# Last attention layer of a four-layer network: the decay table's first step on VectorE, its bias and causal mask on GpSimd, and another order of calls per step

## Chip, cores and metric

The kernel runs on one core of a Trainium2 chip, in one launch. The metric is the device time in microseconds (us) of that launch. Everything is float32. The engines are TensorE (PE in the profile; its weight loads are PEld), VectorE (DVE), ScalarE (ACT), GpSimd (POOL) and the queue SP, which issues DMAs.

## What is computed

Four layers, each a normalisation, an attention, a feed-forward part and a gated sum, over 8 sequences of 512 tokens with 128 channels. The change lies in the attention of the last layer, which the kernel computes for 16 heads of 64 complex channels. Cut to what matters (`B_`=8, `N_`=512, `H_`=16, `DH_`=64):

```python
ang = t[:, None, None] * om[None]
phase = jax.lax.complex(jnp.cos(ang), jnp.sin(ang))
qr = q * phase[None]
kr = k * phase[None]
dt = jnp.abs(t[:, None] - t[None, :])
E = jnp.exp(jnp.clip(-mu[:, None, None] * dt[None], MIN_EXP, 0.0))      # MIN_EXP = -30
s = jnp.einsum('bihd,bjhd->bhij', qr, jnp.conj(kr)).real
V = (sigma_sq / (2.0 * mu))[:, None, None] * (1.0 - E * E) + (eta_sq + gamma_sq)[:, None, None]
maha = jnp.maximum(qn[..., None] + (E * E)[None] * kn[:, :, None, :] - 2.0 * E[None] * s, 0.0) / V[None]
coef = (-0.5 * tau * (nu + DH_))[None, :, None, None]
logits = coef * jnp.log1p(maha / nu[None, :, None, None]) - 0.5 * DH_ * jnp.log(V)[None]
logits = jnp.where(causal[None, None], logits, -jnp.inf)
A = jax.nn.softmax(logits, axis=-1)
out = jnp.einsum('bhij,bjhd->bihd', A.astype(v.dtype), v)
y = jnp.concatenate([out.real.reshape(B_, N_, DKt), out.imag.reshape(B_, N_, DKt)], axis=-1)
return y @ Wo
```

E and V depend on the head and on the distance of two tokens alone, not on the sequence.

## The kernel before

`l3_attention` holds one 512 x 512 causal score matrix as four row tiles of 128 rows with 128, 256, 384 and 512 columns, packed side by side: 1280 columns on 128 partitions. `off` gives the place of each row tile and `w` its width, so the square that the diagonal crosses is the last 128 columns of each row tile. Everything per score is an instruction of 1280 columns, or four instructions, one for each row tile, in the order 3, 2, 0, 1.

**Tables.** For each head, `class Tables` makes three tiles of 128 x 1280, two buffers each. `decay` writes E = max(nmu * dt, -30) on GpSimd, `exp` takes its exponential on ScalarE; `squares` (G = E * E), `variance` and `variance_nu` (V) are GpSimd's; `log` takes ln G on ScalarE; `bias` is one VectorE instruction, G = G * g_v + later, where `later` is a tile made once, 0 where the key is not later than the query and -1e30 elsewhere. So G carries the bias and the causal mask into the logits. A new `Tables` also issues the DMAs of the head's two weights and of its cosines and sines. The first head's tables are made at once, beside the layer norm in front of the attention; those of heads 1 to 15 by the entries "T..." of the step.

**Pairs.** The 128 pieces of work (16 heads x 8 sequences) are taken two sequences at a time: 64 objects of `class Pair`, x = 0 or 1 being the sequence. In the order of the data:
- `project` (PE, keys then queries), `rotate` (DVE: r2 = sin * psum, DMA of r2 to rs with the partition halves exchanged, r = cos * psum), `turned` (GpSimd: r = r + rs), `squares` (ACT), `key_norms`, `query_norms` (PE), `key_lengths` (ACT), `query_lengths` (DVE), `key_terms` (GpSimd: ek = E * kn, four instructions).
- `scores` (PE), `halved` (DVE: sc = -2 sc + ek), `scaled` (DVE: sc = sc * E), `distances` (DVE, four instructions, y = max(sc + qn, V)), `log` (ACT, both x at once), `logits` (DVE, both x: y = coef * y + G, 2560 columns, two inputs in SBUF).
- `maxima i` (DVE, row tile i of both x), `exps x i` (ACT), `inverse` (DVE), `values` (PE, the value and output weights already multiplied) and `keep_values` (ACT), `turn` (PE transposes) and `keep` (ACT), `weigh` (PE, 10 products, 20 passes), `normalise` (ACT), `add` (GpSimd, into the sum over heads). `finish` turns the sum back for the last head.

**Order.** `STEP` is a list of 72 calls. Step t runs it once: "1 scores 0" calls `scores(0)` of pair t+1, "-1 keep 0 2" calls `keep(0, 2)` of pair t-1, and "T2 variance" runs in every fourth step, where t % 4 is 2, for the next head. `in_order` fixes each engine's instructions to that order; the engines wait for each other by semaphores. So one call's place in the list sets only what it stands behind on its own engine, and the DMAs of `rotate` and of a new `Tables` keep their order on SP.

**Buffers that matter.** PSUM: one tile for scores (`s`), one for projections (`kq`), one for weighted sums (`o`), two (`j`) shared in turn by norms, transposes and values. SBUF: one r2, one rs, one sq; two of r, ek, kn, y, o, u and at.

Below, "step" is one run of the list, (n, x) in brackets is pair t+n and sequence x.

Of the kernel before, what the change touches and what calls it, by code (L numbers as in the profile page):

```python
# [9 lines left out]
F32 = mybir.dt.float32  # L10
I32 = mybir.dt.int32
AF = mybir.ActivationFunctionType
ALU = mybir.AluOpType
# [3 lines left out]
P = 128  # L17
# [6 lines left out]
NEG = -1.0e30  # L24
# [1284 lines left out]
def l3_attention(net, x, xn, s_out):  # L1309
    nc, tc = net.nc, net.tc  # L1310
    H, DH = 16, 64
    NQ = S // P
    PK = P * NQ * (NQ + 1) // 2


    w = [P * (i + 1) for i in range(NQ)]
    off = [896, 1024, 512, 0]
    banks = [(0, 512, (3,)), (512, 512, (2, 0)), (1024, 256, (1,))]
    with ExitStack() as st:
        p1 = st.enter_context(tc.tile_pool(name="a3_1", bufs=1))  # L1320
# [4 lines left out]
        sp, nmu, v_e2, v_0, coef, k_0, q_0, g_v = net.prep.scalars  # L1325
# [2 lines left out]
        wvo = p1.tile([P, H, P], F32, tag="wvo", name="wvo")  # L1328

        dt = p1.tile([P, PK], F32, tag="dt", name="dt")  # L1330
        later = p1.tile([P, PK], F32, tag="later", name="later")
        nc.gpsimd.memset(later, 0.0)
        with tc.tile_pool(name="a3_d", bufs=1) as pd:
            di = pd.tile([P, PK], I32, tag="di", name="di")
            for i in range(NQ):
                cols = slice(off[i], off[i] + w[i])
                nc.gpsimd.iota(di[:, cols], pattern=[[-1, w[i]]], base=P * i, channel_multiplier=1)
                nc.gpsimd.affine_select(
                    out=later[:, cols], in_=later[:, cols], compare_op=ALU.is_ge, fill=NEG,
                    base=P * i, pattern=[[-1, w[i]]], channel_multiplier=1,  # L1340
                )
            nc.vector.tensor_copy(dt, di)
        nc.vector.scalar_tensor_tensor(dt, dt, -1.0, dt, ALU.mult, ALU.max)

# [3 lines left out]
        pe, dve, act, pool = (  # L1348
            net.in_order(e) for e in (nc.tensor, nc.vector, nc.scalar, nc.gpsimd)
        )  # L1350
# [8 lines left out]
        class Tables:  # L1359


            def __init__(self, h):
                self.h, self.hs = h, slice(h, h + 1)
                for nm in "qk":
# [14 lines left out]
                nc.sync.dma_start(self.sn[96:128, :], sin)  # L1379
                self.E, self.V, self.G = (  # L1380
                    pw.tile([P, PK], F32, tag=nm, name=nm) for nm in "EVG"
                )

            def decay(self):
                pool.tensor_scalar(self.E, dt, nmu[:, self.hs], -30.0, ALU.mult, ALU.max)

            def exp(self):
                table_set("exp_and_others")
# [2 lines left out]
            def squares(self):  # L1391
                pool.tensor_tensor(self.G, self.E, self.E, ALU.mult)

            def variance(self):
                G = self.G
                pool.tensor_scalar(G, G, v_e2[:, self.hs], v_0[:, self.hs], ALU.mult, ALU.add)

            def variance_nu(self):
                G = self.G
                pool.tensor_scalar(self.V, G, nu[:, self.hs], 1.0, ALU.mult, ALU.mult)  # L1400

# [2 lines left out]
                act.activation(self.G, self.G, AF.Ln)  # L1404

            def bias(self):
                G = self.G
                dve.scalar_tensor_tensor(G, G, g_v[:, self.hs], later, ALU.mult, ALU.add)

        tables = {}  # L1410
        T = tables[0] = Tables(0)
# [2 lines left out]
        with tc.tile_pool(name="a3_v", bufs=2, space=PSUM) as p_v, tc.tile_pool(  # L1414
            name="a3_vw", bufs=2
# [24 lines left out]
        class Pair:  # L1440
# [185 lines left out]


        STEP = (
            "0 scores 1", "-1 exps 0 3", "1 key_lengths 0", "-1 exps 0 0", "-1 turn 0 2",
            "T1 decay", "0 halved 1", "-1 keep 0 2", "1 key_terms 0", "1 query_norms 0",  # L1630
            "-1 turn 0 0", "-1 exps 1 0", "-2 normalise 1", "1 query_lengths 0", "1 project 1 0",
            "1 turned 0", "0 scaled 1", "-1 exps 1 1", "-1 turn 0 1", "0 distances 1",
            "-1 keep 0 0", "1 project 1 1", "-2 add 0", "-1 keep 0 1", "1 rotate 1", "-1 weigh 0",
            "-1 inverse", "-1 turn 1 2", "0 log", "-1 turn 1 1", "0 logits", "T3 log",
            "1 scores 0", "T3 bias", "0 maxima 2", "-1 keep 1 2", "1 squares 1", "-1 keep 1 1",
            "0 values 0", "1 turned 1", "1 key_norms 1", "-1 normalise 0", "2 project 0 0",
            "0 keep_values 0", "1 halved 0", "1 key_lengths 1", "1 query_norms 1", "0 maxima 1",
            "-1 turn 1 0", "1 query_lengths 1", "T2 variance", "2 project 0 1", "0 exps 0 1",
            "0 values 1", "1 key_terms 1", "-1 keep 1 0", "T2 variance_nu", "-2 add 1", "T1 exp",
            "-1 weigh 1", "1 scaled 0", "2 squares 0", "0 maxima 3", "0 exps 1 2", "T1 squares",  # L1640
            "0 exps 1 3", "1 distances 0", "2 rotate 0", "2 key_norms 0", "0 keep_values 1",
            "0 exps 0 2", "0 maxima 0",
        )
        for t in range(-2, N + 3):
            if t + 2 < N:
# [391 lines left out]
def network(tc, ins, out):  # L2037
    with ExitStack() as ctx:
        net = Net(ctx, tc, ins)
        xp = ctx.enter_context(tc.tile_pool(name="acts", bufs=1))  # L2040
        x = xp.tile([P, NT], F32, tag="x", name="x")
        for t in range(NTB):
            tc.nc.sync.dma_start(x[:, ts(t, TB)], ins["x"][:, ts(t, TB)])
        xn = xp.tile([P, NT], F32, tag="xn", name="xn")
        s = xp.tile([P, NT], F32, tag="s", name="s")
        prep = net.prep = Prepared(net, ctx)
        with tc.tile_pool(name="prep_0", bufs=1) as p0:
            net.layer_norm(x, xn)
            l0_attention(net, xn, s)
            prep.l0_decode(p0)  # L2050
            l0_ffn(net, x, xn, s)
        net.layer_norm(x, xn)
        l1_layer(net, x, xn, s)
        net.layer_norm(x, xn)
        with tc.tile_pool(name="prep_t", bufs=1) as pt:
            prep.l2_weights(pt)
            l2_attention(net, xn, s)
            prep.angles(pt)
            prep.l3_scalars()
            l2_ffn(net, x, xn, s)  # L2060
            prep.sines()
        l3_attention(net, x, xn, s)
        l3_ffn(net, x, xn, s, out)
# [76 lines left out]
```

## Time and profile before

| what | us |
|---|---|
| runs of the kernel | 2869.78, 2870.13, 2882.57; median 2870.13 |
| the profiled execution's own time | 2865.32 |
| its span in the trace | 2863.6 |
| attention of the last layer, steady part (first to last `logits`) | 1361.3 to 2683.1 |
| from the last `logits` to the first work after the attention | 2683.1 to 2713.6 |

The span is what the trace covers; 1.7 us of the execution lie around it. In the trace all the calls of `STEP` carry line 82, that of the helper `in_order`, so that instructions are told apart by their tiles: `y<-y,coef,G` is `logits`, `G<-G,g_v,later` is `bias`, `E<-dt,nmu` is `decay`, `s<-s,o` is `add` (the sum over heads lies in s), `r<-r,rs` is `turned`, `ek<-E,kn` is `key_terms`. A row of a timeline reads: start, duration, engine, line, operation, output<-inputs, number of instructions, and in square brackets how long the engine was idle before it and what ended that. Successive VectorE instructions overlap by about 0.09 us, so durations add up to slightly more than the time they take.

### The profile page before, as it was taken

How to read it: one execution, taken by the hardware profiler on the slowest of the kernel's cores; microseconds unless marked ns; L12 is line 12 of the kernel's file. 1: busy time of each engine (PE TensorE's matmuls, PEld its weight loads, DVE VectorE, ACT ScalarE, POOL GpSimd, SP SyncE). 2: the span in 40 equal slices, each digit the busy share in tenths (PEclk: the TensorE clock that was granted, in tenths of full speed). 3: DMA queues.
4: the chain of work that ended last, by engine and by line, in shares of the span. 5: the costliest groups of instructions: out<-in, count | busy, mean ns of one | idle time of the engine just before them, and what ended most of it. 6: DMA issues, size and time to landing. Idle time of an engine off the chain costs nothing. (4 is left out here: it accounts for less than half of the span.)

```text
span 2863.6 us, 48763 instructions
## 1 busy us (share of the span) xinstructions
PE 2575.9 (90%) x18636; PEld 1801.4 (63%) x18636; DVE 2195.4 (77%) x2907; ACT 1835.7 (64%) x3587; POOL 1556.8 (54%) x1262
## 2 busy tenths in 40 slices
PE   7999898688778889977999999999999999999887
PEld 5666666455335555535677777677777777777674
DVE  4777454566663666664999999999999999999565
ACT  2666342245331455452899888898888889888734
POOL 2444221532342333335677877877877787777323
PEclk7999797899898899877999999999999999999989
DMA  1000002112100000003222222222222222222000
GB/s 48 2 2 2 1 1 89 30 51 46 32 28 17 2 2 2 2 23 92 62 61 57 49 62 61 61 61 57 54 57 61 62 56 66 55 52 52 25 1 30
DMA packets 56310, 112.73 MB, mean 39 GB/s; under 512 B 10768, under 2 KB 28752, under 8 KB 55440
## 3 DMA queue, kind: packets, MB, share of 16 engines
q1 hardware_dynamic: 51584, 99.40, 13.2%
q0 software_dynamic: 4352, 8.92, 1.3%
q8 instruction: 148, 2.42, 0.4%
q10 hardware_dynamic: 144, 1.31, 0.1%
q14 instruction: 82, 0.67, 0.1%
HBM read 30.43 MB, written 12.06 MB: 15 GB/s over the span
## 5 line engine op out<-in xcount | busy, mean ns | idle before, releaser
L82 POOL TENSOR_TENSOR ek<-E,kn 128x512 f32<-128x512 f32 (+3 forms) x512 | 427.1, 867 | 63.2 <-ACT kn L82 62.1
L82 POOL TENSOR_TENSOR r<-r,rs 128x1024 f32<-128x1024 f32 x128 | 317.9, 2484 | 252.9 <-DMA rs<-r 213.1
L82 POOL TENSOR_TENSOR e<-e,mx 128x1024 f32<-128x1024 f32 x112 | 212.6, 1898 | 333.8 <-DVE mx L82 195.5
L82 ACT ACTIVATE y<-y,mx 128x256 f32<-128x256 f32 (+3 forms) x512 | 287.2, 562 | 101.2 <-DVE mx L82 101.1
L82 PE MATMUL sc<-r 128*128 128x512 f32 (+3 forms) x1024 | 307.9, 444 | 24.6 <-POOL r L82 18.8
L82 PEld LDWEIGHTS ps_av<-u,at 128*128 128x128 f32 x2560 | 302.3, 193 | 41.2 <-ACT at L82 31.3
L82 PE MATMUL ps_av<-u,at 128*128 128x128 f32 x2560 | 315.1, 279 | 6.5 <-ACT at L82 6.5
L82 PEld LDWEIGHTS sc<-r 128*128 128x128 f32 x1024 | 166.4, 192 | 176.5 <-issue 71.7
L82 DVE SCALAR_TENSOR_TENSOR y<-sc,qn,V 128x512 f32<-128x512 f32 (+3 forms) x512 | 246.0, 543 | 2.3
L82 ACT ACT_TABLE_LOAD x167 | 214.3, 1283 | 4.1 <-PE pa L82 1.2
L82 DVE TENSOR_REDUCE mx<-y 128x2 f32<-128x768 f32 (+3 forms) x256 | 207.7, 812 | 1.7
L82 DVE SCALAR_TENSOR_TENSOR sc<-sc,ek 128x1280 f32<-128x1280 f32 x128 | 191.3, 1495 | 12.5 <-PE sc L82 6.2
L82 PE MATMUL tp<-ident,y 128*128 128x128 f32 x1280 | 198.5, 278 | 1.2 <-ACT y L82 0.8
L82 DVE SCALAR_TENSOR_TENSOR y<-y,coef,G 128x2560 f32<-128x2560 f32 x64 | 195.7, 3058 | 4.6 <-ACT y L82 2.3
L82 ACT COPY at<-tp 128x512 f32<-128x512 f32 (+1 forms) x384 | 188.2, 512 | 7.8 <-PE tp L82 7.7
L82 DVE TENSOR_TENSOR sc<-sc,E 128x1280 f32<-128x1280 f32 x128 | 191.1, 1493 | 0.0
L82 PEld LDWEIGHTS tp<-ident,y 128*128 128x128 f32 x1280 | 154.3, 146 | 41.4 <-issue 18.3
L82 POOL TENSOR_TENSOR s<-s,o 128x512 f32<-128x512 f32 x120 | 162.6, 1356 | 31.1 <-ACT o L82 31.1
L82 PEld LDWEIGHTS ps_u<-wvo,xn 128*128 128x128 f32 x1024 | 128.3, 191 | 69.2 <-DVE qn L82 55.2
L82 DVE TENSOR_TENSOR r<-sn,ps_kq 128x1024 f32<-128x1024 f32 x128 | 154.9, 1210 | 7.6 <-ACT sq L82 4.1
L82 ACT ACTIVATE y<-y 128x2560 f32<-128x2560 f32 x64 | 149.7, 2339 | 15.6 <-DVE y L82 8.1
L82 PE MATMUL tp<-ident,e 128*128 128x128 f32 x896 | 135.0, 294 | 23.6 <-ACT rt L82 14.4
(396 smaller groups left out, 5779.4 us busy)
## 6 DMA issues: line engine op xcount, KB each, us to landing
rs<-r SPq DMA_DIRECT2D x256, 256.0 KB
yrows<-yy SPq DMA_DIRECT2D x36, 128.0 KB
ct<-trig SPq DMA_DIRECT2D x16, 256.0 KB
m_w<-m_w SPq DMA_DIRECT2D x1, 2560.0 KB
x<-x SPq DMA_DIRECT2D x8, 256.0 KB
xrows<-row SPq DMA_DIRECT2D x8, 256.0 KB
sn<-trig SPq DMA_DIRECT2D x32, 64.0 KB
sn<-trig SPq DMA_DIRECT2D x16, 128.0 KB
```

Source lines behind the costliest of these rows:

```text
L82: ins = op(*args, **kwargs)
```

## The change

`decay` goes from GpSimd to VectorE, with the same operands. `bias` goes from one VectorE instruction to five on GpSimd: a product with g_v over all 1280 columns, then on the last 128 columns of each row tile an affine select, which keeps a score where row >= column and writes -1e30 elsewhere. `later`, its memset and its four selects go. `STEP` has the same 72 calls with the table calls at other steps ("T0 decay", "T0 exp" where it was T1) and another order; it starts at another point of the cycle.

```diff
-        later = p1.tile([P, PK], F32, tag="later", name="later")
-        nc.gpsimd.memset(later, 0.0)
         with tc.tile_pool(name="a3_d", bufs=1) as pd:
             di = pd.tile([P, PK], I32, tag="di", name="di")
             for i in range(NQ):
                 cols = slice(off[i], off[i] + w[i])
                 nc.gpsimd.iota(di[:, cols], pattern=[[-1, w[i]]], base=P * i, channel_multiplier=1)
-                nc.gpsimd.affine_select(
-                    out=later[:, cols], in_=later[:, cols], compare_op=ALU.is_ge, fill=NEG,
-                    base=P * i, pattern=[[-1, w[i]]], channel_multiplier=1,
-                )
...
             def decay(self):
-                pool.tensor_scalar(self.E, dt, nmu[:, self.hs], -30.0, ALU.mult, ALU.max)
+                dve.tensor_scalar(self.E, dt, nmu[:, self.hs], -30.0, ALU.mult, ALU.max)
...
             def bias(self):
+
                 G = self.G
-                dve.scalar_tensor_tensor(G, G, g_v[:, self.hs], later, ALU.mult, ALU.add)
+                pool.tensor_scalar(G, G, g_v[:, self.hs], 1.0, ALU.mult, ALU.mult)
+                for i in range(NQ):
+                    last = G[:, off[i] + P * i : off[i] + P * i + P]
+                    pool.affine_select(
+                        out=last, in_=last, compare_op=ALU.is_ge, fill=NEG,
+                        base=0, pattern=[[-1, P]], channel_multiplier=1,
+                    )
...
         STEP = (
+            "1 project 0 1", "0 key_terms 1", "-1 maxima 3", "-2 weigh 1", "-1 values 1",
+            "-1 exps 0 1", "1 squares 0", "-1 exps 1 1", "-1 exps 1 2", "1 key_norms 0",
+            "-1 keep_values 1", "-1 exps 0 3", "0 distances 0", "0 scores 1", "-1 exps 1 3",
+            "-1 turn 0 2", "1 key_lengths 0", "-1 exps 0 2", "-1 keep 0 2", "T1 squares",
+            "T0 decay", "-1 turn 0 0", "T2 variance", "1 rotate 0", "-1 maxima 0", "-1 exps 0 0",
+            "1 query_norms 0", "0 halved 1", "-1 keep 0 0", "0 scaled 1", "1 key_terms 0",
+            "-1 exps 1 0", "1 project 1 0", "-2 normalise 1", "1 query_lengths 0", "1 turned 0",
+            "-1 turn 0 1", "-1 keep 0 1", "1 project 1 1", "0 distances 1", "-1 weigh 0",
+            "1 rotate 1", "0 log", "-1 turn 1 2", "-1 turn 1 1", "-1 keep 1 2", "1 squares 1",
+            "T3 log", "1 scores 0", "-1 inverse", "-1 keep 1 1", "-1 normalise 0", "0 logits",
+            "-2 add 1", "0 maxima 1", "1 key_norms 1", "-1 turn 1 0", "1 key_lengths 1", "T3 bias",
+            "1 turned 1", "1 halved 0", "2 project 0 0", "T2 variance_nu", "-1 keep 1 0",
+            "0 maxima 2", "-1 add 0", "0 values 0", "T0 exp", "0 keep_values 0", "1 query_norms 1",
+            "1 scaled 0", "1 query_lengths 1",
         )
```

In the changed program's order, engine by engine, VectorE's list reads: maxima 3 (-1), distances (0,0), in step T0 decay, rotate (1,0), maxima 0 (-1), halved (0,1), scaled (0,1), query_lengths (1,0), distances (0,1), rotate (1,1), inverse (-1), logits (0), maxima 1 (0), halved (1,0), maxima 2 (0), scaled (1,0), query_lengths (1,1). The number of VectorE instructions stays, GpSimd gets 4 more per head.

## The prediction, on record before the changed kernel ran

> **What bounds it.** I read the page's slices for the stage, the busy times by stretch, VectorE's timeline for the length of a step, and GpSimd's beside it for the excess.
>
> ```profile
> PE   7999898688778889977999999999999999999887
> DVE  4777454566663666664999999999999999999565
> ```
> ```profile
> core 0: us, PE busy (x) PEld busy (x) DVE busy (x) ACT busy (x) POOL busy (x), PEclk, DMA share, GB/s
> 1361.30:2683.10 1321.80, 1283.10 (x7528) 941.65 (x7528) 1302.12 (x1522) 1175.38 (x2477) 1018.04 (x801) 1.00 0.23 58
> 2683.10:2713.60 30.50, 20.97 (x130) 17.45 (x128) 7.47 (x9) 18.09 (x51) 5.97 (x4) 0.89 0.01 1
> ```
>
> In the steady part VectorE is busy 98.5%, PE 97.1, ScalarE 88.9, GpSimd 77.0: VectorE bounds it, PE close behind. Busy time hides waits inside an instruction, so I take the starts of `logits`, one per step:
>
> ```profile
> 1738.47 2.89 DVE L82 SCALAR_TENSOR_TENSOR y<-y,coef,G 128x2560 f32<-128x2560 f32 x1
> ...
> 1758.87 2.88 DVE L82 SCALAR_TENSOR_TENSOR y<-y,coef,G 128x2560 f32<-128x2560 f32 x1
> 1761.67 1.54 DVE L82 SCALAR_TENSOR_TENSOR G<-G,g_v,later 128x1280 f32<-128x1280 f32 x1
> ```
> ```profile
> 1780.60 2.88 DVE L82 SCALAR_TENSOR_TENSOR y<-y,coef,G 128x2560 f32<-128x2560 f32 x1
> ...
> 1800.99 2.88 DVE L82 SCALAR_TENSOR_TENSOR y<-y,coef,G 128x2560 f32<-128x2560 f32 x1
> ...
> 1807.80 0.22 DVE L82 TENSOR_SCALAR qn<-ps_qn,q 128x4 f32<-128x4 f32 x1 [0.94 <-PE ps_qn L82]
> ...
> 1815.37 1.50 DVE L82 SCALAR_TENSOR_TENSOR sc<-sc,ek 128x1280 f32<-128x1280 f32 x1 [0.40 <-POOL G L82]
> ```
>
> A plain step is 20.40 (1738.47 to 1758.87, 1780.60 to 1800.99), VectorE back to back. The step with `bias` is 21.73. The step from 1800.99 ends at 1822.77, 21.78. So each of the 15 heads with tables costs 4 x 20.40 plus 1.33 for `bias` plus some 1.1 to 1.4 more. The 63 steps from the first to the last `logits` (1361.26 to 2683.13) make 1321.87 = 63 x 20.40 + 36.7; `bias` is 15 x 1.33 = 20.0 of that, the rest 16.7. GpSimd shows what the rest is:
>
> ```profile
> 1790.84 4.59 POOL L82 TENSOR_SCALAR E<-dt,nmu 128x1280 f32<-128x1280 f32 x1
> ...
> 1801.12 3.88 POOL L82 TENSOR_TENSOR s<-s,o 128x512 f32<-128x512 f32 x1
> ```
> ```profile
> 1548.88 4.00 DVE L82 SCALAR_TENSOR_TENSOR y<-y,coef,G 128x2560 f32<-128x2560 f32 x1
> ```
> ```profile
> 1548.91 1.29 POOL L82 TENSOR_TENSOR s<-s,o 128x512 f32<-128x512 f32 x1
> ```
>
> `decay` makes GpSimd late, its next `add` meets `logits`, and one of the two stands still: `add` takes 3.88 for its usual 1.28 (and ScalarE, PE, VectorE wait behind it, 0.94 and 0.40), or `logits` takes 4.00 for 2.88. One of these hits every head.
>
> **Edits, each costed on that.**
>
> ```profile
> L82 POOL TENSOR_SCALAR V<-G,sp 128x1280 f32<-128x1280 f32 x16 | 21.4, 1338 | 0.1
> ...
> L1338 POOL TENSOR_SCALAR_AFFINE_SELECT later<-later 128x128 f32<-128x128 f32 x1 | 0.3, 293 | 0.1
> ```
> ```profile
> L82 DVE SCALAR_TENSOR_TENSOR G<-G,g_v,later 128x1280 f32<-128x1280 f32 x16 | 24.8, 1548 | 0.1
> ...
> L1342 DVE CAST dt<-di 128x1280 f32<-128x1280 int32 x1 | 0.8, 817 | 0.0
> ```
> ```profile
> L1981 DVE TENSOR_SCALAR ang<-tt,a_om x4: 474/474/1367, 1246.5 to 1249.3; 128x512 f32<-128x512 f32 x4
> ```
>
> 1. `bias` leaves VectorE: -15 x 1.33 = -20.0.
> 2. `decay` leaves GpSimd, and the hit above goes: -16.7. The GPSIMD Engine Reference of the Trainium skill (4.1, Engine selection) says one-input work there runs at about line rate; V's 1.34 agrees, `decay` of the same shape, with a maximum in it, takes 4.59. By the rule only 1.3 per head would leave GpSimd and the late `add` would be unexplained; I go by the row. What is next late on GpSimd comes in 4.
> 3. `decay` on VectorE: the cast of this shape takes 0.82; a one-pointer product of 512 columns takes 0.474 where one with constants takes 0.42, so 0.82 + 0.05 = 0.87, less 0.09 overlap: 15 x 0.78 = +11.7.
> 4. `decay` against GpSimd. The page SBUF — State Buffer (Who interferes with whom) says a one-source VectorE instruction in its fast mode locks GpSimd's port, and who starts first keeps it for that instruction. The 1367 in the last row fits: 0.9 over its fellows, beside a GpSimd sum. Where is GpSimd then? In step T3 `bias` needs G from ScalarE's T3 log, which ends at 15.3 on the clock below, and is held by `logits` to 16.0; product and selects (1.34 + 4 x 0.29, less overlaps) end at 18.4, `turned` at 20.8, `add` at 22.0, key_terms(0,1) (3.3) at 25.3, which is 4.9 of step T0. `decay` comes at 2.96, in the middle. By the page it waits for the rest of one key_terms instruction, at most 1.0 (their means are 1.27, 1.00, 0.46, 0.73). By the row it waited for a whole queued one too: `logits` came 0.1 before a `turned` ended, yet `add` went first. Bounds: 0 (GpSimd idle) to 1.9 (all of key_terms). I take 1.1, nearest to the stretched `logits`. The first head's comes before GpSimd is loaded: 14 x 1.1 = +15.4.
> 5. GpSimd's new 2.4 per head costs nothing: it was 77% busy and loses 4.6. Behind `bias` stand turned(1,1), needed by scores(0,1) at 23.6 and there at 20.8, and key_terms(0,1), needed by `halved` at 6.4 of T0 and there at 4.9 to 5.8. If that cover is gone, VectorE waits up to 2.4 per head.
> 6. The order. I lay VectorE's new list end to end from `maxima 3` at 0, by start-to-start times of the old timeline: distances(0,0) 1.12, [T0 decay 2.96], rotate(1,0) 2.96, maxima 0 5.21, halved(0,1) 5.65, scaled 7.19, distances(0,1) 8.72, rotate(1,1) 10.56, inverse 12.8, logits 13.04, maxima 1 15.96, halved(1,0) 16.55, scaled(1,0) 18.8, end 20.4. No VectorE instruction is added in a plain step. The tight waits:
>  - scores(0,1) start 0.14 after distances(0,0) ends and take 2.40: 5.6, 0.05 before `halved`. The old order has the same loop with the same work in it, and holds 20.40.
>  - PE's pieces sum to 19.63, so 0.77 spare. key_norms(1,1) must wait for squares(1,1), which ScalarE does after `log`, 14.2; PE then reaches scores(0,1) with 0.46 spare. In T3 the G log puts PE 0.5 late, which `decay` in T0 covers.
>  - ScalarE: keep(-1,0,1) ends 8.85, table load 10.2, `log` is due at 10.67: 0.45 spare.
>  - GpSimd: rs lands 4.4 after r2 (8.6), turned(1,0) 11.0, `add` 12.2, 0.8 before `logits`.
>  All close, so I take 0 for the order in a plain step, with -0.1 to +0.3 a step as bounds. The new weight loads go on SP behind the same rotations: 0.
> 7. Start of the attention: ScalarE stood still for GpSimd's `decay` in front of the layer norm's squares, and the layer norm's next GpSimd power stood behind it (1307.5 to 1310.1):
>
> ```profile
> 1310.06 1.27 ACT L82 ACTIVATE E<-E 128x1280 f32<-128x1280 f32 x1 [5.45 <-POOL E L82]
> ```
>  With `decay` done on VectorE at about 1306.8, that power starts 2.5 sooner: -2.5. scaled(0,0) no longer stands behind a `qn` that waited 1.26: -1.0. The memset and selects of `later` lay in idle time: 0.
> 8. The end: 27.6 lie between the end of the last `logits` and 2713.6. In the new order ScalarE's chain of exponentials, copies and one `normalise` is 8.2 long before the last weigh 0, where the old one started it 11.5 after (2697.58). Then 2.5 + turns and copies 5.8 + 2.5 + normalise, add, turn, copy 3.7: 22.7. So -5, bounds 0 and -8.
>
> Sum: -20.0 - 16.7 + 11.7 + 15.4 - 3.5 - 5 = -18.1. On the profiled execution's 2865.3: 2847.2. The median of the runs is 4.8 above it, carried over: **2852**, -0.63%. A measurement of this kernel can tell about 0.5% from no change: 2855.8 and 2884.5 are the limits.
>
> **Rivals.**
> - A, the above: 2852. For it: every number is a row. Against: slacks of half a microsecond.
> - B, `decay` finds GpSimd idle, because key_terms runs earlier than I place it: 15.4 comes back, 2837. For it: my place for key_terms is off by 2 at most to miss. Against: in T3 GpSimd has 13.9 + 2.4 to do and starts `bias` late.
> - C, `decay` waits for all four key_terms, and the end wins nothing: 14 x 0.8 + 5 = +16, 2868. For it: the stretched `logits` lost to a queued instruction. Against: there it lost only one.
> - D, PE becomes the bound, and it is slower: key_norms(1,1) waits for squares(1,1) behind `log`, and with values(0,0) behind key_lengths(1,1), in the shared two `j` buffers. It decides once these waits pass the 0.77 that PE has spare; each 0.1 over costs 63 x 0.1 = 6.3, and from 0.29 over the gain is gone. At 0.55 over: +35, 2887. For it: PE is 97% busy and the T3 step already overruns. Against: in my layout 0.46 is left.
>
> **Chances.** A 0.42, B 0.18, C 0.24, D 0.16. A lies 4 us inside the limit: 0.30 of it falls faster, 0.12 same. B is faster, C same, D 0.13 slower and 0.03 same. Faster 0.48, same 0.39, slower 0.13. Range: up into D and down to B's middle, 2835 to 2877, which leaves out about 0.08 below and 0.11 above. A's own range is 2845 to 2860, by the bounds of `decay`'s wait and the end.
>
> **What would show it.** Starts of `logits`: 20.40 in three steps of four, 22.3 from T3 to T0. `E<-dt` on VectorE 0.87 alone, about 2 in the trace for heads 2 to 15 (B: 0.87, C: 2.8). No `logits` over 2.9, no `add` over 1.4. `bias` on GpSimd 2.4, starting with the end of `logits`. D would show as VectorE waiting for PE's `sc` in every step. Wrong altogether if plain steps are not 20.40.

## Result and profile after

| | before | after |
|---|---|---|
| runs, median us | 2869.95 (2868.86 to 2882.57, 4 runs) | 2842.98 (2828.71 to 2848.09, 4 runs) |
| ratio | | 0.9899, 95% interval 0.9864 to 0.9934 |
| profiled execution, its span | 2865.32, 2863.6 | 2848.09, 2846.4 |

The change makes the kernel 1.0% faster. The prediction was 2852.

The two profiled executions differ by 17.2, less than the 27 of the medians. A cut of the span at four instructions that both kernels have says why. The cuts are: the layer norm's second `var` in front of the attention, the first `logits`, the last `logits`, and the first sums of the next layer norm.

| stretch, us | before | after | difference |
|---|---|---|---|
| span's start to second `var` (unchanged code) | 1297.80 | 1305.35 | +7.55 |
| start of the attention, to the first `logits` | 63.46 | 56.41 | -7.05 |
| steady part, first to last `logits` | 1321.87 | 1302.51 | -19.36 |
| end, last `logits` to the next layer norm | 30.99 | 28.67 | -2.32 |
| behind it (unchanged code) | 149.48 | 153.46 | +3.98 |

The three changed stretches give -28.7, as the ratio does (0.0101 x 2870 = 29). The unchanged stretches are not equally long in all executions: over the 14 traces of this case the second `var` lay between 1286.5 and 1305.4, with the same code in front of it. So from here on the changed stretches are compared one by one.

The page's slices after. PE and VectorE carry the steady part as before:

```profile
PE   7999898678678799987999999999999999999887
DVE  4777464566663666665999999999999999999565
```

Busy times by stretch, for the steady part and the end. The clock that TensorE was granted is the third figure from the end of a row:

```profile
core 0: us, PE busy (x) PEld busy (x) DVE busy (x) ACT busy (x) POOL busy (x), PEclk, DMA share, GB/s
1361.76:2664.27 1302.51, 1277.34 (x7529) 940.96 (x7528) 1287.16 (x1522) 1182.32 (x2477) 976.73 (x861) 1.00 0.23 58
2664.27:2692.94 28.67, 20.10 (x130) 17.10 (x129) 7.99 (x10) 18.78 (x52) 5.99 (x4) 0.88 0.02 3
```

VectorE is busy 1287.2 of 1302.5, 98.8%, and still bounds it. GpSimd fell from 1018.0 to 976.7, PE is 98.1%.

"A step from T3 to T0" below is the time from the `logits` of a step where t % 4 is 3 to those of the next one. VectorE's timeline around such a step, with two rows of the step before it in front:

```profile
1581.02 0.41 DVE L82 TENSOR_REDUCE mx<-y 128x2 f32<-128x256 f32 x1
1581.49 1.50 DVE L82 SCALAR_TENSOR_TENSOR sc<-sc,ek 128x1280 f32<-128x1280 f32 x1
...
1588.89 2.88 DVE L82 SCALAR_TENSOR_TENSOR y<-y,coef,G 128x2560 f32<-128x2560 f32 x1
...
1599.16 1.40 DVE L82 TENSOR_SCALAR E<-dt,nmu 128x1280 f32<-128x1280 f32 x1
...
1602.74 0.41 DVE L82 TENSOR_REDUCE mx<-y 128x2 f32<-128x256 f32 x1
1603.07 1.48 DVE L82 SCALAR_TENSOR_TENSOR sc<-sc,ek 128x1280 f32<-128x1280 f32 x1
...
1610.46 2.88 DVE L82 SCALAR_TENSOR_TENSOR y<-y,coef,G 128x2560 f32<-128x2560 f32 x1
```

`logits` starts 21.57 apart (1588.89 to 1610.46). 47 of the 63 steps are 20.39 to 20.41; 13 from T3 to T0 are 21.54 to 21.57, one is 21.43, the first step of all is 20.95, and the step into the last head's pairs, behind which no further `decay` stands, is 21.02. `decay` takes 1.40 and the next instruction starts 1.32 after it. The rows of `mx` and `sc` show a small wait to be used again below: from this `maxima` to `halved` it is 0.47 in the plain step and 0.33 here, so a plain step holds 0.14 of waiting for PE's scores.

GpSimd beside it:

```profile
1591.29 1.69 POOL L82 TENSOR_SCALAR G<-G,g_v 128x1280 f32<-128x1280 f32 x1 [3.19 <-ACT G L82]
1593.06 1.05 POOL L82 TENSOR_SCALAR_AFFINE_SELECT G<-G 128x128 f32<-128x128 f32 x4
...
1597.62 3.94 POOL L82 TENSOR_TENSOR ek<-E,kn 128x512 f32<-128x512 f32 x4
```

`bias` on GpSimd takes 1.69 and 1.05, 2.7 in all, and begins 0.48 before `logits` ends (1591.77). Then `turned`, `add`, and at 1597.62 key_terms(0,1), in which `decay` falls: its four instructions take 3.94, in plain steps 3.34.

The groups of the trace, over all 16 heads, the first one's tables in front of the steady part included (busy us, mean ns of one):

```profile
L82 POOL TENSOR_SCALAR G<-G,g_v 128x1280 f32<-128x1280 f32 x16 | 26.7, 1667 | 49.1 <-ACT G L82 49.1
...
L82 DVE TENSOR_SCALAR E<-dt,nmu 128x1280 f32<-128x1280 f32 x16 | 21.7, 1358 | 0.0
```

No `logits` lasts over 2.89 now (mean 3.06 before), and the mean `add` is 1.29 (1.36 before): the collision is gone that had made 13 of the 15 steps from T1 to T2 last 21.36 to 21.82 before.

### The profile page after: what moved, and what is told of

Same layout as the page of the kernel before. It is cut to its first block, busy times and chain, and to the rows that moved or that the text cites. A ratio compares the mean times of both kernels' runs of the same rounds, so it can differ in the third digit from the quotient of the medians.

```text
span 2846.4 us, 49014 instructions
## 1 busy us (share of the span) xinstructions
PE 2569.6 (90%) x18636; PEld 1798.8 (63%) x18636; DVE 2182.7 (77%) x2907; ACT 1843.5 (65%) x3587; POOL 1509.8 (53%) x1321
## 5 line engine op out<-in xcount | busy, mean ns | idle before, releaser
L82 POOL TENSOR_TENSOR ek<-E,kn 128x512 f32<-128x512 f32 (+3 forms) x512 | 435.6, 886 | 47.2 <-ACT kn L82 47.2
L82 POOL TENSOR_TENSOR r<-r,rs 128x1024 f32<-128x1024 f32 x128 | 302.5, 2363 | 237.0 <-DMA rs<-r 212.1
L82 PE MATMUL ps_av<-u,at 128*128 128x128 f32 x2560 | 308.8, 276 | 3.1 <-ACT o L82 3.1
L82 ACT COPY at<-tp 128x512 f32<-128x512 f32 (+1 forms) x384 | 198.6, 517 | 42.1 <-PE tp L82 40.9
L82 DVE TENSOR_REDUCE mx<-y 128x2 f32<-128x512 f32 (+3 forms) x256 | 207.5, 812 | 2.2
L82 PE MATMUL tp<-ident,y 128*128 128x128 f32 x1280 | 183.7, 274 | 9.3 <-ACT at L82 7.5
L82 DVE SCALAR_TENSOR_TENSOR y<-y,coef,G 128x2560 f32<-128x2560 f32 x64 | 184.6, 2885 | 5.3 <-ACT y L82 2.7
L82 POOL TENSOR_TENSOR s<-s,o 128x512 f32<-128x512 f32 x120 | 155.1, 1292 | 29.8 <-ACT o L82 29.8
L82 DVE TENSOR_TENSOR r<-ct,ps_kq 128x1024 f32<-128x1024 f32 x128 | 155.3, 1213 | 0.0
```

Source lines behind the costliest of these rows:

```text
L82: ins = op(*args, **kwargs)
```

## The experiments

Theory A is the prediction's: the gain comes from which engine does what; the order costs and gains nothing in plain steps; what is left in the step from T3 to T0 is `decay` with a wait for GpSimd, over a lateness of PE that the T3 log makes. The rivals are that the order alone makes the gain, that it is the order that makes the engines' exchange possible, and that the lateness isn't there. All times are of the profiled execution of each kernel; ratios are to the kernel before in the same set of runs.

| kernel | ratio, 95% interval | start | steady | end | step T3 to T0 |
|---|---|---|---|---|---|
| before | | 63.5 | 1321.9 | 31.0 | 21.73 to 21.86 (T1 to T2: 21.4 to 21.8 in 13 of 15) |
| after | 0.9899 (0.9864 to 0.9934) | 56.4 | 1302.5 | 28.7 | 21.57 |
| new engines, old order | 0.9919 (0.9894 to 0.9945) | 55.2 | 1305.0 | 29.9 | 20.61, then 21.43 |
| old engines, new order | 1.0046 (1.0031 to 1.0060) | 62.7 | 1340.9 | 27.3 | 21.9 to 25.4 |
| `decay` back on GpSimd | 1.0054 (1.0034 to 1.0074) | 62.8 | 1337.4 | 28.6 | 21.01, then 21.2 to 24.4 |
| `bias` back on VectorE | 1.0038 (1.0022 to 1.0054) | 55.8 | 1343.3 | 30.0 | 24.3 |
| no `decay` | 0.9892 (0.9859 to 0.9925) | 56.0 | 1296.9 | 28.2 | 21.02 |
| log later | 0.9890 (0.9862 to 0.9918) | 56.3 | 1304.4 | 27.9 | 21.70 |
| no `decay`, log later | 0.9877 (0.9841 to 0.9912) | 56.3 | 1296.8 | 28.3 | 21.02 |
| `decay` before `logits` | 0.9907 (0.9880 to 0.9934) | 52.5 | 1305.2 | 27.3 | 21.65 |
| log and bias moved, no `decay` | 0.9842 (0.9814 to 0.9870) | 56.2 | 1286.6 | 28.6 | 20.47 |
| log, bias, `decay` moved | 0.9867 (0.9834 to 0.9901) | 53.3 | 1294.0 | 28.1 | 21.03 |
| final copies on VectorE | 0.9895 (0.9857 to 0.9933) | 53.2 | 1302.8 | 26.7 | 21.55 |
| log and bias moved, no `decay`, final copies on VectorE | 0.9831 (0.9802 to 0.9860) | 56.2 | 1286.6 | 28.0 | 20.47 |

**New engines in the old order.** The changed kernel with the `STEP` of before.

```diff
-            "1 project 0 1", "0 key_terms 1", "-1 maxima 3", "-2 weigh 1", "-1 values 1",
...
+            "0 scores 1", "-1 exps 0 3", "1 key_lengths 0", "-1 exps 0 0", "-1 turn 0 2",
+            "T1 decay", "0 halved 1", "-1 keep 0 2", "1 key_terms 0", "1 query_norms 0",
...
```

> The changed kernel's engines (decay on VectorE, bias with selects on GpSimd) in the order of calls of before (decay in step T1 behind scores(0,1), bias in T3 in front of turned(1,1)). Measured so far from first to last logits: 1321.9 before, 1302.5 after. Theory A, the engines make the gain and any order that feeds VectorE will do: about 1303 to 1310, plain steps 20.40, the total within 8 us of the changed kernel (2843 to 2851). Rival, the gain hangs on the new order because the old one puts bias in front of turned(1,1) and VectorE waits up to 2.4 us a head for its scores: up to 1321.9 - 36.7 + 14 x 1.3 + 15 x 2.4 = 1339, slower than before (2885).

Theory A holds: 1305.0, and a ratio that cannot be told from the changed kernel's. The step from T3 to T0 pays 0.21, because `halved` waits 0.28 for its scores. GpSimd's `bias` is not what makes them late: `turned`, behind it, ends at 1580.53, and PE, busy without a gap since 1575.83, starts them only at 1583.78. PE had waited 0.20 and 0.24 for copies of ScalarE that stand behind the table's log. The step with `decay` pays 1.03: there `decay` takes 1.25 at 1606.46, because GpSimd has begun key_terms(1,0) at 1605.76. So in the steady part the exchange of engines is worth 16.9, and the new order 2.5 on top, of which 1.7 lie in the old order's very last step (22.12).

**Old engines in the new order.**

```diff
-            "0 scores 1", "-1 exps 0 3", "1 key_lengths 0", "-1 exps 0 0", "-1 turn 0 2",
...
+            "1 project 0 1", "0 key_terms 1", "-1 maxima 3", "-2 weigh 1", "-1 values 1",
...
```

> The kernel before, its engines unchanged (decay on GpSimd, bias one VectorE instruction with the mask tile), in the new order of calls. Theory A, the order alone gains nothing: bias keeps its 15 x 1.33 = 20 and GpSimd, late by decay's 4.59, still holds something up every head (0.5 to 1.1): first to last logits 1313 to 1322, total 2860 to 2872. Rival, the new order alone makes the gain by putting GpSimd's late instructions where they meet nothing: 1285 + 20 = 1305 or less, total under 2850.

Neither: the order alone loses 19 in the steady part. I had expected a gain of 0 to 9 for theory A, so one thing was missing in it. The kernel with `bias` back on VectorE, below, shows it.

**`decay` back on GpSimd.**

```diff
-                dve.tensor_scalar(self.E, dt, nmu[:, self.hs], -30.0, ALU.mult, ALU.max)
+                pool.tensor_scalar(self.E, dt, nmu[:, self.hs], -30.0, ALU.mult, ALU.max)
```

> The changed kernel with decay back on GpSimd at the same place of the new order, bias still on GpSimd. Theory A: GpSimd gets 4.6 a head in step T0, between key_terms(0,1) and key_terms(1,0), which makes turned(1,0) about 4 late for scores(1,0); PE has 0.8 to give, so T0 steps rise from 21.57 to 22.5 to 24.5; first to last logits 1315 to 1343, total 2856 to 2884. Rival, GpSimd takes it up in its idle time (it is 74% busy) and VectorE loses decay's 1.3: T0 steps near 21.0, 1295, total 2836.

1337.4, within theory A's range, but in another place: the step from T3 to T0 is 21.01, and the one after it pays up to 4.0. VectorE's row, then GpSimd's rows of the same stretch, in such a step:

```profile
1615.69 4.15 DVE L82 SCALAR_TENSOR_TENSOR y<-y,coef,G 128x2560 f32<-128x2560 f32 x1
```

```profile
1614.80 2.35 POOL L82 TENSOR_TENSOR r<-r,rs 128x1024 f32<-128x1024 f32 x1
1617.11 3.85 POOL L82 TENSOR_TENSOR s<-s,o 128x512 f32<-128x512 f32 x1
```

GpSimd, late by its 4.59, is in `turned` when `logits` comes at 1615.69. `logits` waits for the rest of it (1.42, to 1617.11) and then runs its 2.7; the `add` queued behind `turned` stands still until `logits` is over and takes 3.85 for 1.29. So the running GpSimd instruction is finished, and then VectorE goes first. The same happens in 13 heads (`logits` 4.14 to 4.16).

**`bias` back on VectorE**, with the mask tile `later` of before.

```diff
-                pool.tensor_scalar(G, G, g_v[:, self.hs], 1.0, ALU.mult, ALU.mult)
-                for i in range(NQ):
...
+                dve.scalar_tensor_tensor(G, G, g_v[:, self.hs], later, ALU.mult, ALU.add)
```

> The changed kernel with bias back on VectorE as one instruction with the mask tile. Theory A: T3 steps +1.2 to +1.33 (15 x = 18 to 20); GpSimd has its 2.7 a head back, so key_terms(0,1) is over before decay, which then takes 0.88 in place of 1.40 (14 x 0.5 = -7): first to last logits 1302.5 + 18 to 20 - 7 = 1313 to 1316, if decay still waits 1320 to 1322. Rival, bias on VectorE falls into a wait for PE (the T3 log makes PE late) and costs under 0.7 a head: 1303 to 1306.

1343.3: my 1313 to 1322 was far off, the rival's 1303 further. VectorE's rows, then GpSimd's:

```profile
1588.44 3.35 DVE L82 SCALAR_TENSOR_TENSOR G<-G,g_v,later 128x1280 f32<-128x1280 f32 x1
...
1598.46 0.87 DVE L82 TENSOR_SCALAR E<-dt,nmu 128x1280 f32<-128x1280 f32 x1
```

```profile
1588.09 2.35 POOL L82 TENSOR_TENSOR r<-r,rs 128x1024 f32<-128x1024 f32 x1 [3.99 <-DMA rs<-r]
1590.39 2.53 POOL L82 TENSOR_TENSOR s<-s,o 128x512 f32<-128x512 f32 x1
```

`bias` reads two tiles in SBUF. In the new order it stands behind `maxima`, and there it meets `turned`: it waits 1.95 for the rest of that and lasts 3.35 for its 1.4 to 1.5. 3.27 from start to start and 0.79 for `decay`, less the 0.14, are 3.92 over 20.40: the measured 24.32. In the old order it stood directly behind `logits`, before `turned`, and took 1.54. This goes far to explain the old engines in the new order too: their `bias` has a mean of 3.02, for 1.55 before, and 15 x 1.47 = 22 is of the size of the 19 lost. And one part of the expectation held: with GpSimd free of `bias`, key_terms is over in time and `decay` takes 0.87 where it took 1.40.

**No `decay`**, to see what lies under it.

```diff
-                dve.tensor_scalar(self.E, dt, nmu[:, self.hs], -30.0, ALU.mult, ALU.max)
+                pass
...
-                act.activation(self.E, self.E, AF.Exp)
+                act.activation(self.E, dt, AF.Exp, scale=nmu[:, self.hs])
```

> The changed kernel without decay as an instruction: the exponential reads dt with scale nmu, so the clip at -30 is left out. ScalarE's exponential stays as long as it was. The changed kernel's step from T3 to T0 is 21.57, that of the last head, which has no decay, 21.02. Theory A, beneath decay lies PE's lateness from the T3 log: all T3 to T0 steps become 21.02; first to last logits 1302.5 - 14 x 0.55 - 0.5 = 1294 to 1295. Rival, the lateness is the last head's alone and decay pays the whole 1.17: 20.40 throughout, 1286.

21.02 in all 15 heads: `decay` costs 0.55 a head and not 1.17, since PE's lateness of 0.62 lies under it. (1.1 of the 2 over the expected 1295 are the first step of all, 22.08 for 20.95.)

**Log later**, and **no `decay`, log later.**

```diff
-            "T3 log", "1 scores 0", "-1 inverse", "-1 keep 1 1", "-1 normalise 0", "0 logits",
+            "1 scores 0", "-1 inverse", "-1 keep 1 1", "T3 log", "-1 normalise 0", "0 logits",
```

> The changed kernel with the T3 log moved two ScalarE instructions later, behind keep(-1,1,1), so that this copy and PE's turn(-1,1,0) no longer wait for it. Theory A: the last head's step goes from 21.02 to 20.40, the other T3 to T0 steps stay 21.57 since decay with its wait for the port is longer; first to last logits 1302 (-0.6 in all). Rival, the log still makes something late (normalise, and weigh behind it): the last head's step stays above 20.7. If decay and PE's lateness add up: 21.57 goes to 21.0, 1294.

> Both of the last two: no decay instruction (the clip at -30 is left out) and the T3 log behind keep(-1,1,1). Theory A: every step 20.40, first to last logits 1285.2 to 1287, 16 below the changed kernel; the total some 2827. Rival, another wait takes their place (GpSimd's key_terms, weigh): steps from T3 to T0 stay at 20.7 to 21.0, 1290 to 1295.

Theory A fails in both: the last head's step stays 21.02, and `decay` even pays 0.13 more (it takes 1.53, as GpSimd's `bias` comes later). I had named the wrong follower of the log. The trace of the second kernel names the right one; ScalarE, PE and VectorE of one step from T3 to T0:

```profile
1590.02 1.30 ACT L82 ACTIVATE G<-G 128x1280 f32<-128x1280 f32 x1
...
1592.19 0.73 ACT L82 ACTIVATE kn<-ps_kn,k 128x512 f32<-128x512 f32 x1
```

```profile
1592.97 1.16 PE L82 MATMUL ps_u<-wvo,xn 128*128 128x128 f32 x8 [0.76 <-ACT kn L82]
```

```profile
1602.13 1.50 DVE L82 SCALAR_TENSOR_TENSOR sc<-sc,ek 128x1280 f32<-128x1280 f32 x1 [0.68 <-issue]
```

The log still stands ahead of key_lengths(1,1) (1592.19). values(0,0) on PE needs the PSUM buffer that this call frees, and PE is 0.76 idle for it. All that follows on PE is late: the scores end at 1602.03, and `halved` has waited 0.68 for them. GpSimd's `bias` is no rival here, since what stands behind it was in time: `turned` ended at 1596.19, the scores started at 1599.71, and key_terms(0,1) ended at 1600.73.

**`decay` before `logits`**, where GpSimd is idle.

```diff
-            "T0 decay", "-1 turn 0 0", "T2 variance", "1 rotate 0", "-1 maxima 0", "-1 exps 0 0",
+            "-1 turn 0 0", "T2 variance", "1 rotate 0", "-1 maxima 0", "-1 exps 0 0",
...
-            "T3 log", "1 scores 0", "-1 inverse", "-1 keep 1 1", "-1 normalise 0", "0 logits",
+            "T3 log", "1 scores 0", "-1 inverse", "T0 decay", "-1 keep 1 1", "-1 normalise 0",
...
```

> The changed kernel with decay moved within step T0 from behind distances(0,0) to in front of logits, where GpSimd has nothing to do (13.9 to 17.4 us after maxima 3). Theory A, decay was there to fill VectorE's wait for PE: it takes 0.88 and no longer 1.40, but now stands behind that wait; T3 to T0 steps 21.02 + 0.79 = 21.8 (was 21.57), first to last logits 1305 to 1306. Rival, the wait for GpSimd's port was the whole loss: 21.57 - 0.52 = 21.05, 1295.

Theory A: 1305.2, step 21.65. `decay` takes 0.84 (mean) and meets nothing, and the step is still longer than the changed kernel's, because it now comes after PE's lateness and not in its place: 21.02 + 0.63. A wait of 0.5 for the port, in a gap that VectorE has anyway, was the cheaper of the two.

**Log and bias moved.** ScalarE's log goes behind keep(-1,1,0), where in other steps the table's exponential stands, and so behind key_lengths(1,1); GpSimd's `bias` goes behind key_terms(0,1) of the next step ("U0": the same head, one step on), where step T1 has `squares`.

```diff
-            "1 project 0 1", "0 key_terms 1", "-1 maxima 3", "-2 weigh 1", "-1 values 1",
+            "1 project 0 1", "0 key_terms 1", "U0 bias", "-1 maxima 3", "-2 weigh 1", "-1 values 1",
...
+            "1 halved 0", "2 project 0 0", "T2 variance_nu", "-1 keep 1 0", "T3 log", "0 maxima 2",
...
-                if n[0] == "T":
-                    h = t // 4 + 1
-                    if t >= 0 and t % 4 == int(n[1]) and h < H:
+                if n[0] in "TU":
+                    h = t // 4 + (n[0] == "T")
+                    if h >= 1 and t >= 0 and t % 4 == int(n[1]) and h < H:
```

> No decay instruction (the exponential reads dt with scale nmu, the clip at -30 is left out), the T3 log five ScalarE instructions later, behind keep(-1,1,0), where other steps have the table's exponential, and bias behind key_terms(0,1) of the next step, where step T1 has GpSimd's squares. Theory A, the 0.62 left in the step from T3 to T0 is values(0,0) waiting for key_lengths(1,1), which stood behind the log wherever it was tried: that step becomes 20.40, first to last logits 1285 to 1289, total some 2826. Rival, the 0.62 comes from GpSimd's bias in front of turned(1,1): it goes too, and cannot be told apart here, or it stays because bias now holds key_terms(1,0): 21.0, 1297.

> The whole computation: the changed kernel with log and bias placed as in the last one, and decay in front of logits in step T0, where GpSimd is idle. Theory A: T3 to T0 steps 20.40 + 0.63 to 0.79 = 21.0 to 21.2, first to last logits 1294 to 1297, total some 2835, faster than both kernels. Rival, with the log later another wait appears (bias ends at 12.5 of 20.4, and decay in front of logits delays the rest): 21.57 or more, 1302 or more.

The second kernel also has "T0 decay" in front of `logits` as above. Without `decay` it is 1286.6, that is 63 x 20.40 + 1.4: of the tables 0.07 a head is left (20.47). This and the trace above make the log the cause; `bias` moved along, and no run moves the log alone as far as this. With `decay`, in front of `logits`, it is 1294.0, 8.5 below the changed kernel for the whole computation. The first kernel's 20.47 and this one's 21.03 differ by 0.56; `decay` takes 0.75 of VectorE, from its start to that of `logits`:

```profile
1518.68 0.84 DVE L82 TENSOR_SCALAR E<-dt,nmu 128x1280 f32<-128x1280 f32 x1
1519.43 2.88 DVE L82 SCALAR_TENSOR_TENSOR y<-y,coef,G 128x2560 f32<-128x2560 f32 x1
```

**Final copies on VectorE**, alone and on top of the first of the last two.

```diff
-                act.copy(s_out[:, ts(self.b + x, S)], tp)
+                copy = act.copy if self.b == 0 else dve.tensor_copy
+                copy(s_out[:, ts(self.b + x, S)], tp)
```

> The changed kernel with the last three pairs' final copies (finish) on VectorE in place of ScalarE. From the last logits to the next layer norm's first sums: 28.67 now (27.3 to 29.9 over the runs in the new order). Theory A, ScalarE's table load and exponentials stood behind two of these copies (1.08 and a wait of 0.71 for PE): 1.5 to 2 less, 26 to 27. Rival, PE at its low clock sets the end (weigh took 4.63 for 2.40): unchanged, 27.5 to 29.

> The first kernel of this set (no decay instruction, so the clip at -30 is left out, log and bias moved) with the final copies on VectorE. Theory A: both gains, first to last logits 1285 to 1289, the end 26 to 27, total some 2824. Rival: the end as it was, 28, total 2826.

ScalarE at the end of the changed kernel, and of this one:

```profile
2668.20 1.08 ACT L82 COPY s<-tps 128x512 f32<-128x512 f32 x2 [0.71 <-PE tps L82]
2669.30 1.28 ACT L82 ACT_TABLE_LOAD   x1
```

```profile
2661.31 0.58 ACT L82 COPY u<-ps_u 128x512 f32<-128x512 f32 x1 [0.31 <-PE ps_u L82]
2661.92 1.28 ACT L82 ACT_TABLE_LOAD   x1
```

The two copies of pair 61 stood in front of the table load and the exponentials; without them the load starts 0.61 behind the copy of u in place of 2.39. But then ScalarE waits for PE's next values, which it did not before:

```profile
2666.18 0.58 ACT L82 COPY u<-ps_u 128x512 f32<-128x512 f32 x1 [1.27 <-PE ps_u L82]
```

So weigh(0) starts 12.68 behind the start of the last `logits`, where the changed kernel has 13.09: 0.41 of the 1.95 by which the end became shorter (28.67 to 26.72). Another part is PE's pace, which is the rival: weigh(0) took 4.02 here and 4.63 in the changed kernel. Of the kernels in the new order that keep the copies, two had weigh(0) at 3.9 and an end of 27.3, and six had it at 4.63 and an end of 28.1 to 28.7 (left out is the one with `bias` back, where weigh(0) starts later still). On top of the other edits weigh(0) took 4.63 as well, and the end is 27.98, 0.1 to 0.7 below those six. So both held in part: the copies are worth 0.7 at most, and the greater part of the 1.95 is PE's pace.

With everything the ratio is 0.9831, 2819 where the kernel before had 2869 in the same set; this one leaves out the clip. Its interval lies below the changed kernel's, though they were measured in different sets; the one with the whole computation is at 0.9867, and its interval overlaps the changed kernel's.

## Why the prediction was right, and what was off in it

The predicted time was 2852, the measured one 2843; in the changed stretches -18.1 was forecast and -28.7 came. The steady part gave 9.8 more than forecast, the start 3.6 more and the end 2.7 less, so the misses cancel in part. By the prediction's own steps:

- **1 and 2, `bias` and the collision leave (-36.7):** right. Plain steps are 20.40, no `logits` lasts over 2.89, and in the trace nothing is left of either. The prediction did not see that the two moves belong together: either one taken back in the new order costs 35 to 41.
- **3, `decay` on VectorE, 0.87 alone:** measured 0.87 and 0.84. Right.
- **4, the wait for GpSimd, 1.1 a head (+15.4): the term that was mis-sized.** The place was right to 0.01 (2.96 after `maxima 3`: 1596.20 to 1599.16) and so was key_terms (1.4 to 5.4 for 1.6 to 4.9). The wait is 1.40 - 0.87 = 0.53. I had weighed the Trainium skill's page SBUF — State Buffer (Who interferes with whom: an exclusive lock, the one that starts first keeps it for its instruction) against a row and gone by the row: the stretched `logits` at 1548.88, beside an `add` that started at 1548.91, read as losing to a queued instruction. Those starts are 0.03 apart: it was a dead heat that GpSimd won, and so it was in eight stretched `logits` before (0.03 to 0.05 apart) and for the `decay` at 1350.73 after, which took 1.46. How such a tie is settled is not shown. Wherever VectorE came while a GpSimd instruction was still running for longer (1615.69, 1588.44, `decay` in two orders) it lost the rest of that one and no more. The rule was right, with what it leaves unsaid: the waiting VectorE instruction goes ahead of GpSimd's next.
- **3 and 4 together** were 1.88 a head, so steps of 22.3; measured 1.17. 0.57 of the difference is the wait, 0.14 is the plain step's own wait for scores, which `decay` fills. 14 x 0.71 = 9.9 is about the whole miss of the steady part (-9.6 forecast, -19.4 measured). The T3 log's lateness "which `decay` in T0 covers" was 0.62 where 0.5 was forecast, and it was covered, as the kernel without `decay` shows.
- **5, GpSimd's 2.4 cost nothing:** 2.7, hidden, but `decay` meets key_terms because of it; with `bias` back, it did not.
- **6, the order at 0 in plain steps:** right, 20.40. Of D, the rival on the slower side, nothing is seen.
- **7, the start, -3.5:** -7.05. The cause was right and half of the size: GpSimd's power now starts 0.25 after its `var`, before 2.81 after it. With that PE, which had stood still for it, runs faster too. Rows of the same 16 products, before and after:

```profile
1311.82 3.78 PE L101 MATMUL ps<-ident,rstd 128*128 128x128 f32 x16 [3.60 <-POOL rstd L113]
```

```profile
1317.92 2.05 PE L101 MATMUL ps<-ident,rstd 128*128 128x128 f32 x16 [1.01 <-POOL rstd L113]
```

From the third `var` to the fourth it is 13.34 before and 6.67 after. All eleven kernels without `decay` on GpSimd have a start of 52.5 to 56.4; the three with it there, the kernel before among them, one of 62.7 to 63.5.
- **8, the end, -5:** -2.3. The step that failed is the chain of 8.2 on ScalarE. From the table load to weigh(0) it is 8.1, but the load starts 2.15 after the end of the last `logits`, behind the final copies of pair 61, which the prediction left out; so weigh(0) came 10.2 after that end. Without the copies PE's values would have held it nearly as long, as the run with them on VectorE shows. weigh(0) itself was taken at 2.5 where it ran 4.63, as it already did before the change (at 2697.58); turns and copies behind it took 4.0 for 5.8, so that the two together, 8.7 for 8.3, miss by little.

The rivals: B (`decay` finds GpSimd idle, 2837) had the wrong mechanism and yet lay nearer in time, 6 off, than A, 9 off: the total alone does not choose between them, the 1.40 does. It also excludes C (`decay` waits for all of key_terms).

## What to carry to other kernels

When an instruction is moved to the engine that is the bound, place it where that engine waits for another one anyway: then only what it is longer than that wait costs. When two engines share a port, price a meeting as the rest of the instruction that is running, and look for a pair of start times before reading more into a stretched one. An order of calls belongs to its placement on engines: here the new order with the old engines was 19 us slower in the steady part, although it gained 2.5 with the new ones.

## What the runs showed of the hardware that I had not expected

PE at half pace. The same 16 products took 3.78 behind a gap of 3.60 and 2.05 behind one of 1.01; weigh, 2.40 in the steady part, took 4.63 once in the end. The granted clock (the third figure from the end) tells them apart, first the 16 products before:

```profile
core 0: us, PE busy (x), PEclk, DMA share, GB/s
1311.82:1315.60 3.78, 3.78 (x18) 0.50 0.09 36
```

and after, with weigh(1) and weigh(0) of the end:

```profile
1317.92:1319.97 2.05, 2.05 (x19) 1.00 0.26 61
2668.44:2670.84 2.40, 2.40 (x24) 1.00 0.01 3
2677.36:2681.99 4.63, 4.63 (x21) 0.50 0.00 0
```

The Trainium skill's page TensorE: Matmul & The Clock Gate (Part 1) describes such a gate: half rate after an idle window of about 3.4 us that runs freely. The length of one gap does not decide here: the next 16 products took 3.68 (clock 0.54) behind a gap of 1.22 in the changed kernel and 2.05 behind one of 1.21 to 1.22 in four others, and in the 6 us before weigh(0) no gap was over 1.57. A window that runs freely could make such a difference, but no run here isolates it. So an estimate for the ends of a pipelined stage, where PE stands still again and again, needs both prices.
